# A bidirectional scan block on one core: the main loop written as a table of 24 pairs, with matmuls of like tile shape put together

## The chip, the core and the metric

The kernel runs on one core of a Trainium2 chip. A core has TensorE (matmuls, PE in the profile, with PEld for its weight loads), VectorE (DVE), ScalarE (ACT), GpSimd (POOL) and SyncE (SP, which here issues nearly all DMAs). The metric is device microseconds from start to end of one execution. The median of 3 runs before the change is 1835.07 us (1831.49 to 1840.69).

## What is computed

The input x is (4, 128, 96, 96): batch, channels, image. A group norm over 32 groups comes first. Each image is then read as a sequence of 9216 positions in four directions (rows forward and back, columns forward and back), and each sequence goes through the same block:

```python
t = grouped1x1(x, in_proj_w, in_proj_b, 4)        # 128 -> 512 channels
u, gate = t[:, :256], t[:, 256:]
u = silu(u)
u = depthwise_conv(u, dw_w)                       # 5 taps along the sequence
s = conv1x1(u, ssm_in_w)                          # 256 -> 32
a = 0.999 + 0.0009 * sigmoid(conv1x1(u, ssm_delta_w, ssm_delta_b))
bb = tanh(conv1x1(u, ssm_b_w, ssm_b_b)); cc = tanh(conv1x1(u, ssm_c_w, ssm_c_b))
prefix = cumsum(log(a))
hst = exp(prefix) * cumsum(bb * s * exp(-prefix))
u = u + conv1x1(cc * hst + ssm_d * s, ssm_out_w)  # 32 -> 256
u = grouped1x1(u * sigmoid(gate), mix_w, mix_b, 4)
y = conv1x1(u, out_proj_w, out_proj_b)            # 256 -> 128
```

The four directions' outputs are put back in image order, joined (4 x 128 channels), multiplied by fuse_w (512 -> 128), and added to x.

## The kernel before

mix, out_proj and fuse are linear and follow each other, so at the start they are multiplied into one weight, w_fin, one for each direction. The decay and the cumulative sums are one recurrence, h = a*h + b*s, done by VectorE's scan.

**Work units.** There are 8 phases: for each of 4 images first the columns (V), then the rows (H). A phase runs two directions at once, the streams s = 0 and s = 1, one of which is read backwards. It has 6 steps (st) of 1536 positions, and a step is cut by position modulo R = 4 into four parts p of N = 384 columns. A *pair* is both streams of one part: 24 pairs to a phase, 192 in all. Channels are on the partitions; the 256 hidden channels are two halves j.

In the second half of a phase the two streams meet the stretches that the other one has already read. silu outputs and gates are then not computed again: they were written to DRAM (`kept_sil`, `kept`) and are loaded back. `fresh(step)` is true in the first half; `mirror(n)` is not None for pairs whose gates are loaded.

**A pair's way through the engines**, with its lines:

- in_proj (`in_proj`, matmuls by the helper `mm`, L134): 32x32 tiles of the array, 16 for each pair. `silu` L495 on ScalarE. Only in fresh steps, four pairs ahead.
- convolution of the first 128 channels on TensorE. Positions are interleaved by 4, so a five-tap window touches two columns of four-position blocks. `conv` multiplies the block that holds most taps (128x32 tiles, weights `band`); `conv_less` the block that holds the others (64x32 tiles, weights `less`). For p = 0 and p = 3 only one of the four positions of that second block has a tap, for p = 1 and 2 two have. ScalarE copies the result to `u` (L632, L634).
- convolution of the other 128 channels as five taps: the first on ScalarE (L649), four on VectorE (L651), in the PSUM banks TAPS = 0 and 1.
- `proj`: the four small projections (128x32 tiles), then tanh, copy, tanh on ScalarE (L683, L684, L689); `decay` L691 and a product L692 on GpSimd; `scale_s` L701 on ScalarE; `scan` L718 on VectorE.
- six pairs later (LAG): `outputs` L724, L725, L727 on GpSimd; `under` L528 copies u into the banks SSM = 0 to 3; `out_of` L520 adds ssm_out to it (32x128 tiles, four products); where gates are computed, `gate` L514 (32x128 tiles) and tanh L537; `gating` L600 on VectorE multiplies. Banks 0 and 1 serve both the taps and stream 0's ssm_out.
- one pair later still: `accumulate`, sixteen w_fin matmuls in two banks (128x32 tiles), ScalarE copies to `ys` (L751, L753), GpSimd adds it to the image accumulator `acc` (L770).

**What sets the order.** The order is written by hand (`manual_schedule`): every engine runs its instructions in the order in which the code issues them. `pair(t)` issues everything of one turn: convolution and projection of pair t, in_proj of pair t + 4, gates and ssm_out of pair t - 6, w_fin of pair t - 7. Its branches `with_front`, `old`, `ahead` choose between three arrangements, and `late` one at a change of batch, when `acc` has to be sent and loaded anew. `start()` computes the statistics and the first step; `tail()` finishes the last pairs. The statistics of the next batch are computed in small pieces in between (`stats_finish`, a generator that `stats_piece` advances).

At the start SP issues the loads of x (`load_x`), whose chunks VectorE takes statistics of (L282); ScalarE's queue issues the weights small, fuse and main. `stay_busy` are matmuls whose result is not used.

## Time and profile before

| | us |
|---|---|
| median of 3 runs | 1835.07 |
| profiled execution, run time | 1833.3 |
| its span | 1831.6 |
| TensorE busy | 1806.8 |
| ScalarE busy | 1566.0 |
| VectorE busy | 1448.8 |
| GpSimd busy | 1423.5 |

The span runs from the first to the last instruction; the run's time also holds what lies around it. Busy times of different engines lie beside each other. The granted TensorE clock was 0.996 over the span. A row of the page such as

```profile
L520 PE MATMUL psum<-t,main 32*128 32x384 f32 x1536 | 241.9, 513 | 3.3 <-ACT psum L528 2.6
```

reads: line, engine, operation, output and inputs, the tile of the array (rows * columns), shape, count; then busy time in us and the mean of one in ns; then idle time of the engine just before, and what ended most of it. A matmul of the program stands in this trace as two records (768 ssm_out products, 1536 records). The mean of one says little, since tiles of the array work at the same time: what counts is from the start of one group to the start of the next.

### The profile page before, as it was taken

The page shows a single profiled execution, that of the slowest core. Times are in us where ns is not written, and L with a number is a line of the kernel's source. Part 1 is how long each engine was busy: PE and PEld are TensorE (multiplying, and loading weights), DVE is VectorE, ACT ScalarE, POOL GpSimd, SP SyncE. Part 2 cuts the span into 40 slices and gives each one's busy share as a digit, 9 for nine tenths or more (in the row PEclk, how much of TensorE's full clock was granted, in tenths as well). Part 3 has the DMA queues.
Part 4 walks back from the last instruction along what each step waited for, and adds up shares of the span by engine and source line. Part 5 has one row for each costly group of instructions (what it writes and reads, how often), then busy time and mean ns, then how long its engine had stood idle before and what let it go on. Part 6 is the DMA issues. An engine that isn't in the chain of part 4 may idle for free.

```text
span 1831.6 us, 57282 instructions
## 1 busy us (share of the span) xinstructions
PE 1806.8 (99%) x24068; PEld 653.9 (36%) x24068; DVE 1448.8 (79%) x1451; ACT 1566.0 (86%) x2762; POOL 1423.5 (78%) x1469
## 2 busy tenths in 40 slices
PE   7999999999999999999999999999999999999998
PEld 4333333333333333333333333333333333333333
DVE  5888878877878888877778888877877778777886
ACT  4888888988888888888898888888888888888975
POOL 2487887778777888787877888787877788887785
PEclk8999999999999999999999999999999999999999
DMA  6755563444965566244696546443476634535434
GB/s 196 200 191 179 164 192 108 161 144 147 307 227 181 167 188 190 102 142 140 214 296 207 165 162 211 136 152 110 162 236 223 234 123 152 192 109 179 148 122 156
DMA packets 147825, 321.18 MB, mean 175 GB/s; under 512 B 14192, under 2 KB 115696, under 8 KB 147568
## 3 DMA queue, kind: packets, MB, share of 16 engines
q1 hardware_dynamic: 147136, 316.56, 53.1%
q8 instruction: 190, 3.11, 0.7%
q10 hardware_dynamic: 432, 0.96, 0.1%
q14 instruction: 67, 0.55, 0.1%
HBM read 185.21 MB, written 132.25 MB: 173 GB/s over the span
## 4 chain that ended last, share of the span: by engine, by line
PE 96%; ACT 2%; DMA 1%; DVE 1%; issue 0%; SPq 0%; POOL 0%; ACTq 0%; DVEq 0%; POOLq 0%
PE psum L134 82%; PE psum L520 8%; PE psum L514 5%; ACT sil L495 0%; DMA x_in<-in_xs 0%; DMA fuse<-in_fuse 0%; PE psum L286 0%; DVE u L600 0%; ACT t L701 0%; ACT t L689 0%; PE psum L364 0%; ACT psum L649 0%; DMA out<-acc 0%; ACT u L632 0%; DVE psum L651 0%
## 5 line engine op out<-in xcount | busy, mean ns | idle before, releaser
L651 DVE SCALAR_TENSOR_TENSOR psum<-sil,small,psum 128x768 f32<-128x768 f32 x576 | 588.9, 1022 | 33.2 <-ACT psum L649 7.4
L600 DVE SCALAR_TENSOR_TENSOR u<-gate,psum 128x768 f32<-128x768 f32 x376 | 349.6, 952 | 256.6 <-ACT gate L537 118.6
L134 PE MATMUL psum<-u,w_fin 128*32 128x384 f32 x6176 | 551.7, 487 | 0.2 <-ACT t L689 0.2
L134 PE MATMUL psum<-u,main 128*32 128x384 f32 x6144 | 536.4, 490 | 0.1
L770 POOL TENSOR_TENSOR acc<-ys,acc 128x384 f32<-128x384 f32 x374 | 412.2, 1122 | 33.3 <-ACT ys L751 9.1
L724 POOL TENSOR_TENSOR t<-t,t 64x384 f32<-64x384 f32 x191 | 234.9, 1230 | 158.4 <-PE psum L514 78.8
L134 PEld LDWEIGHTS psum<-u,w_fin 128*32 128x32 f32 x6176 | 189.1, 110 | 320.8 <-issue 218.7
L134 PEld LDWEIGHTS psum<-u,main 128*32 128x32 f32 x6144 | 181.6, 110 | 327.6 <-issue 199.1
L528 ACT COPY psum<-u 128x768 f32<-128x768 f32 x352 | 276.9, 800 | 20.7 <-DVE u L651 10.2
L691 POOL TENSOR_SCALAR t<-tm 64x384 f32<-64x384 f32 x191 | 177.0, 927 | 151.0 <-ACT tm L683 100.8
L134 PE MATMUL psum<-sil,band 128*32 128x384 f32 x3072 | 286.8, 489 | 3.1 <-ACT ys L753 3.1
L725 POOL TENSOR_TENSOR t<-t,t 64x384 f32<-64x384 f32 x191 | 246.4, 1290 | 15.0
L520 PE MATMUL psum<-t,main 32*128 32x384 f32 x1536 | 241.9, 513 | 3.3 <-ACT psum L528 2.6
L649 ACT ACTIVATE psum<-sil,small 128x768 f32<-128x768 f32 x192 | 174.1, 907 | 63.2 <-DVE u L600 53.7
L537 ACT ACTIVATE gate<-psum,bnorm 128x384 f32<-128x384 f32 x384 | 192.6, 582 | 28.9 <-PE psum L514 26.9
L692 POOL TENSOR_TENSOR t<-t,tm 64x384 f32<-64x384 f32 x192 | 195.0, 1016 | 15.4 <-ACT t L684 0.2
L651 DVE SCALAR_TENSOR_TENSOR u<-sil,small,psum 128x768 f32<-128x768 f32 x192 | 194.9, 1015 | 7.8
L495 ACT ACTIVATE sil<-psum,bnorm 128x385 f32<-128x385 f32 x384 | 191.7, 584 | 3.6 <-PE psum L134 1.4
L134 PE MATMUL psum<-sil,less 64*32 64x384 f32 x3072 | 168.2, 495 | 0.0
L514 PE MATMUL psum<-x_in,wn 32*128 32x384 f32 x768 | 162.0, 528 | 2.3 <-ACT u L632 1.2
L753 ACT COPY ys<-psum 128x384 f32<-128x384 f32 x281 | 129.9, 476 | 30.2 <-PE psum L134 29.2
L134 PEld LDWEIGHTS psum<-sil,band 128*32 128x32 f32 x3072 | 90.2, 109 | 175.6 <-issue 94.1
(92 smaller groups left out, 1500.3 us busy)
## 6 DMA issues: line engine op xcount, KB each, us to landing
sil<-sil SPq DMA_DIRECT2D x128, 770.0 KB, 6.7
kept<-gate SPq DMA_DIRECT2D x80, 768.0 KB, 3.7
gate<-kept SPq DMA_DIRECT2D x76, 768.0 KB, 5.2
x_in<-in_xs SPq DMA_DIRECT2D x192, 96.2 KB, 2.4
out<-acc SPq DMA_DIRECT2D x48, 384.0 KB, 8.0
acc<-in_xr SPq DMA_DIRECT2D x38, 384.0 KB, 6.9
xs<-in_xr SPq DMA_DIRECT2D x72, 192.0 KB, 4.7
x_in<-in_xs SPq DMA_DIRECT2D x184, 48.1 KB, 3.7
```

Source lines behind the costliest of these rows:

```text
L134: nc.tensor.matmul(o[r, : rhs.shape[-1]], lhsT, rhs, start=start, stop=stop, skip_group_check=True)
L495: nc.scalar.activation(sils[step][:, s, j, g, :], bank(bk)[:, : N + 1], AF.Silu, bias=bn[:, 1:2] if j else bn[:, 4 + g : 5 + g],)
L514: nc.tensor.matmul(bank(to)[:, :N], stats[un["b"]][0][r, s, :], x_in[s][r, q, off : off + N], start=True, stop=True)
L520: nc.tensor.matmul(bank(SSM + 2 * s + j)[:, :N], w_so[r, bass.ts(j, P)], z[r, :], start=bi not in seeded, stop=True, skip_group_check=True)
L528: nc.scalar.copy(psum[:, SSM + 2 * s : SSM + 2 * s + 2, :N], us[bi][:, s])
L537: nc.scalar.activation(gv[:, s, j, :], bank(to[2 * s + j])[:, :N], AF.Tanh, bias=bn[:, 2 + j : 3 + j], scale=0.5,)
L600: nc.vector.scalar_tensor_tensor(v, g, 1.0, pz, ALU.add, ALU.mult)
L651: nc.vector.scalar_tensor_tensor(us[i][:, :, 1, :] if k == K - 1 else part, src, w_tap[:, k : k + 1], part, ALU.mult, ALU.add,)
L692: nc.gpsimd.tensor_mul(ta[0:64, p, :], tb[0:64, :], tm[0:64, :])
L724: engine.tensor_mul(ta[0:64, p, :], tb[64:P, :], ta[64:P, p, :])
L725: engine.tensor_add(tb[0:64, :], ta[0:64, p, :], tb[0:64, :])
L770: adder.tensor_add(part, y, part)
```

## The change

The turns t = 6 to 187 are no longer issued by `pair(t)` but read from a table. `ORDER` has 24 rows, one for each pair of a phase; each token is an operation and the pair it belongs to, relative to the row: B0, B1 (conv of a stream), L (conv_less of both), CU (copy to u), FT, T1 to T4 (taps), P (a product of proj), TA, CS, TC (its evictions), DE, BS, SC, SN (decay, product, scale_s, scan), CH, AD, CZ (outputs), X and Z (in_proj and silu), G and H (gate and its tanh), U, S, V (under, ssm_out, gating), A (an add in place of under), W, Y, Q (w_fin, its eviction, its add to acc), BN (statistics). `BANKS` gives each row's PSUM banks and two flags, whether ssm_out and gates are issued as four pieces of 32 columns or as one of 128. `middle()` walks the table, `work()` issues one token. Turns 0 to 5 and 188 to 191, `start()` and `tail()` stay as they were, apart from what is shown.

The order of p within a step becomes (0, 3, 1, 2) in the first half of a phase and (1, 2, 0, 3) in the second. The rows of the array that p = 0 and p = 3 use in `conv_less` are laid out (`ROWS`) so that the two streams of both lie on four different groups of 32 rows; these products are now 32x32 tiles (`lone`), and those of p = 1 and 2 stay 64x32. The weights of the convolution, 22 blocks, are laid out by the host (`band_of`) accordingly.

w_fin's adds (Q) go through a list `held`, which is emptied at once except near a change of batch, where up to three wait. acc is sent and loaded in one piece a turn. `ys` gets 6 buffers in place of 2, `u` one more. At the start the loads of fuse and main move to SP's queue, main behind all of x; the next step's first rows are loaded before the second burst of in_proj; the four `stay_busy(512)` go; the bias product sums w_of and w_fuse over the directions on GpSimd first, so that it has 3 matmuls in place of 12.

```diff
+YS = 6
+FIRST, LAST = 6, 188
+LAGS = {**dict.fromkeys("XZ", -R), **dict.fromkeys("SGHUVA", LAG), **dict.fromkeys("WYQ", LAG + 1)}
+TURNS = ((1, 2, 0, 3), (0, 3, 1, 2))
+ROWS = (((1, 0, 3, 2), (3, 2, 1, 0)), ((0, 1, 2, 3), (2, 3, 0, 1)))
...
+ORDER = (
+    (
+        "B0+1 B1+1 LO+1 DE-1 U1-6 T1 T2 T3 CU+1 LO SC-1 B1 B0 W0-7 T4 CU Q1-8 SN X11+4 X00+4 "
+        "U0-6 X10+4 S10-6 S00-6 S01-6 S11-6 V0-6 Y0-7 Z00+4 CH-5 X01+4 V1-6 P10 P11 Z10+4 "
+        "FT+1 T1+1 T2+1 T3+1 Q0-7 TC Z11+4 AD-5 P00 P01 CS Z01+4 W1-7 TA W0-6 CZ-5 DE Y1-7 "
+    ),
+    (
+        "T4 Q1-8 W1-7 U1-6 Y0-7 SN X00+4 U0-6 Y1-7 S10-6 Z00+4 S11-6 X10+4 X01+4 S00-6 S01-6 "
...
+BANKS = (
+    ((4, 7), (4, 7), (5, 2), (7, 5, 4, 6), (), 1, 1),
...
-            for p in range(R):
+            for turn, p in enumerate(TURNS[st < NS // 2]):
...
-    w_out_fuse = load(fuse, "fuse", pp)
-    load_x([(10, 4)])
-    w_main = load(main, "main")
-    load_x([(14, 4), (18, 4), (22, 2)])
+    w_out_fuse = load(fuse, "fuse", pp, nc.sync)
+    load_x([(10, 4), (14, 4), (18, 4), (22, 2)])
+    w_main = load(main, "main", wp, nc.sync)
...
-        low = 64 * ((less_of(p) + s + 1) % 2)
-        return slice(low, low + 64)
-
-    band = wp.tile([P, 2, R, 4, 32], F32, name="band")
-    less = wp.tile([P, R, 4, 32], F32, name="less")
+        return half(s if p == 1 else 1 - s)
+
+    bands = wp.tile([P, 22, 4, 32], F32, name="band")
+    band = bands[:, 0:16].rearrange("p (f s e) g m -> p f s e g m", f=2, s=2)
+    less = bands[:, 16:20].rearrange("p (f s) g m -> p f s g m", f=2)
+    lone = bands[:, 20:22]
...
+    shape = [P, 4, 32]
+    for e in (8, 12, 21, 11, 15, 9, 13, 18, 19, 10, 14, *range(8), 16, 17, 20):
+        nc.gpsimd.tensor_mul(
+            bands[:, e],
+            id32.unsqueeze(1).broadcast_to(shape),
+            w_dw[:, e, :].unsqueeze(2).broadcast_to(shape),
+        )
...
-    terms = [(w_of[:, d, j, :], b_mix[:, j : j + 1]) for d in range(4) for j in range(2)]
-    terms += [(w_fuse[:, d, :], b_out) for d in range(4)]
+    for w in (w_of, w_fuse):
+        for e in (2, 1):
+            nc.gpsimd.tensor_add(w[:, 0:e], w[:, 0:e], w[:, e : 2 * e])
+    terms = [(w_of[:, 0, j, :], b_mix[:, j : j + 1]) for j in range(2)]
+    terms += [(w_fuse[:, 0, :], b_out)]
...
-    for _ in range(4):
-        stay_busy(512)
...
+        if step > 1 and step % NS != 1:
...
+    def conv_less(i, banks, first=(False, False)):
         step, p = units[i]["step"], units[i]["p"]
-        sil, k, b0 = blocks(step), less_of(p), min(banks)
+        sil, k, f = blocks(step), less_of(p), fresh(step)
         for g in range(4):
             for s in range(2):
-                r = less_rows(s, p)
-                mm(bank(b0 + s), g, less[r, p, g, :], columns(step, sil[s][r, g, :], k),
-                   False, True)
-        if banks == PROJ:
+                if p in (0, R - 1):
+                    row = ROWS[f][s][p]
+                    r = slice(32 * row, 32 * row + 32)
+                    w = lone[r, f, g, :]
+                else:
+                    r = less_rows(s, p)
+                    w = less[r, f, s, g, :]
+                mm(bank(banks[s]), g, w, columns(step, sil[s][r, g, :], k), first[s],
+                   not first[s])
...
+        us[i] = wk.tile([P, 2, 2, N], F32, tag="u", bufs=LAG + 3, name=f"u_{units[i]['id']}")
...
+            ys = wk.tile([P, N], F32, tag="ys", bufs=YS, name=f"ys_{bu['id']}")
...
+    def piece(o, cols, lhsT, rhs, start):
+        nc.tensor.matmul(o[cols, : rhs.shape[-1]], lhsT[:, cols], rhs, start=start, stop=True,
+                         skip_group_check=True)
+
+    def split(small):
+        return [slice(32 * c, 32 * c + 32) for c in range(4)] if small else [slice(0, P)]
...
+        elif kind == "L":
+            conv_less(i, conv_b, [first_of("conv", n, q) for q in range(2)])
+        elif op == "CU":
+            copy_u(i, conv_b)
...
+        elif kind == "S":
+            r = slice(64 * j + 32 * s, 64 * j + 32 * s + 32)
+            for cols in split(s_small):
+                piece(bank(SSM + 2 * s + j), cols, w_so[r, bass.ts(j, P)], tbs[i][r, :], i not in seeded)
...
+        elif kind == "G":
+            q, off = gate_at(units[i])
+            r = slice(64 * (1 - s) + 32 * j, 64 * (1 - s) + 32 * j + 32)
+            for cols in split(g_small):
+                piece(bank(g_b[2 * s + j]), cols, stats[units[i]["b"]][0][r, s, :],
+                      x_in[s][r, q, off : off + N], True)
...
+        elif kind == "W":
+            final_mm(units[i + e], w_b[e])
+        elif kind == "Y":
+            while held and len(adds) >= YS:
+                add_held()
+            adds[n, e] = summand(units[i + e], w_b[e])
...
+        elif kind == "Q":
+            held.append((n, e))
+            turn = 2 * (n % (NU // 2 // B)) + e
+            while len(held) > (max(0, min(turn + 1, 3, 6 - turn)) if n >= NU // 2 // B else 0):
+                add_held()
+        elif kind == "X":
+            step, g = divmod(n, R)
+            in_proj(step, g, s, j, x_b[2 * s + j])
...
+    def slot_begins(t):
+        m = t + R
+        step, g = divmod(m, R)
+        if step * UB < NU and not fresh(step):
+            front(m, None)
+        for n in soon:
+            load_kept(n)
+        soon.clear()
+        if t % (NU // 2 // B) == 0:
+            load_chunks(t + 2)
+        reload_acc(1)
+        send(1)
...
+    def middle():
+        for t in range(FIRST - 2, LAST + 2):
+            if FIRST <= t < LAST:
+                plan_of.append(("", 0, t))
+            for token in ORDER[t % NP].split():
+                op, sign, n = token.partition("+") if "+" in token else token.partition("-")
+                n = t + int((sign + n) or 0)
+                if belongs(op, n):
+                    plan_of.append((op, n, t_of(op, n)))
+        while plan_of:
+            op, n, t = plan_of.popleft()
+            if op:
+                if next_kind[0] is False and free[0] in banks_of(op, t):
+                    stats_piece(False, True)
+                work(op, n, t)
+            else:
+                slot_begins(t)
...
+        for s in range(2):
+            load_front(1, s, slice(64 * s, 64 * s + 32), slice(0, R))
...
-        for t in range(NU // 2):
+        for t in range(FIRST):
+            pair(t)
+        middle()
+        waiting[:] = units[2 * (LAST - LAG - 1) : 2 * (LAST - LAG)]
+        for t in range(LAST, NU // 2):
```

## The prediction

> **What bounds the kernel now.** I read the page's busy shares first, then the chain that ended last, then TensorE's timeline over one pair of each kind.
>
> ```profile
> PE 1806.8 (99%) x24068; PEld 653.9 (36%) x24068; DVE 1448.8 (79%) x1451; ACT 1566.0 (86%) x2762; POOL 1423.5 (78%) x1469
> PE 96%; ACT 2%; DMA 1%; DVE 1%; issue 0%; SPq 0%; POOL 0%; ACTq 0%; DVEq 0%; POOLq 0%
> ```
>
> The first line is busy time by engine, the second the chain by engine: TensorE is the chain nearly throughout, so a microsecond taken from it counts until another engine is late. A busy TensorE need not be a full one; the timeline (start, length, engine, line, instructions) shows what it is busy with. A pair with an in_proj and kept gates:
>
> ```profile
> 244.75 2.79 PE L134 MATMUL psum<-u,main 128*32 128x384 f32 x32
> 247.47 0.95 PE L134 MATMUL psum<-x_in,wn 32*32 32x385 f32 x32
> 248.35 1.50 PE L134 MATMUL psum<-sil,band 128*32 128x384 f32 x16
> 249.66 2.76 PE L134 MATMUL psum<-u,w_fin 128*32 128x384 f32 x32
> 252.36 0.88 PE L134 MATMUL psum<-sil,less 64*32 64x384 f32 x16
> 253.16 0.93 PE L520 MATMUL psum<-t,main 32*128 32x384 f32 x8
> 254.02 2.79 PE L134 MATMUL psum<-u,main 128*32 128x384 f32 x32
> ```
>
> A pair that computes gates:
>
> ```profile
> 330.82 2.79 PE L134 MATMUL psum<-u,main 128*32 128x384 f32 x32
> 333.43 1.47 PE L134 MATMUL psum<-sil,band 128*32 128x384 f32 x16
> 334.72 1.47 PE L134 MATMUL psum<-u,w_fin 128*32 128x384 f32 x16
> 336.12 0.88 PE L134 MATMUL psum<-sil,less 64*32 64x384 f32 x16
> 336.93 1.50 PE L134 MATMUL psum<-u,w_fin 128*32 128x384 f32 x16
> 338.36 0.59 PE L514 MATMUL psum<-x_in,wn 32*128 32x384 f32 x2
> ...
> 339.94 0.53 PE L134 MATMUL psum<-u,main 128*32 128x384 f32 x4
> ```
>
> I count in passes: one pass is the whole array filled once with 384 columns, so four 128x32 tiles, eight 64x32, four 32x128 or sixteen 32x32. The program's 12034 matmuls stand in the trace as two records each, so eight records of 128*32 are a pass. Band to w_fin, 333.43 to 334.72, is two passes of one shape: 1.29 us, 0.645 each. The first pair takes 254.02 - 244.75 = 9.27 us for 13 passes (8.385), so 0.885 us goes to its five changes of tile shape, 0.177 each. The second takes 9.12 for 13 passes with four changes, 0.184 each. So a change of shape costs 0.18 us, and a small product alone in its shape about 0.81 to 0.88 us for 0.645 of work.
>
> **What the Trainium skill says.** "TensorEngine Tiling (Array Packing)", Tiling Modes, says that a change of tiling mode drains the engine while tiles of one mode run independently; the 0.18 us per change agrees. Its Restrictions and Gotchas add that different row tiles must not write one PSUM bank at once; the new table's bank lists keep them apart. "ScalarE: Activation LUTs", What ACT_TABLE_LOAD costs, says that back-to-back ACTIVATEs overlap by about 93 ns. The trace agrees: four silus in a row take 2.00 us, one alone 0.58, so 0.11 is lost per silu that is set apart.
>
> **The change part by part.** Counting tile shapes in the order of both programs gives 2509.0 passes and 867 visits (runs of one shape) before, 2455.7 and 640 after.
>
> *Small conv products.* Pairs with p = 0 and p = 3 now read only the 32 rows in which they have a tap. Both pairs' sixteen 32x32 tiles cover the array once: one pass instead of two, 48 passes over 192 pairs, 48 x 0.645 = 31.0 us. Pairs with p = 1 and 2 keep a full pass each but share a visit.
>
> *in_proj with ssm_out.* Both are now 32x32 in most slots (an ssm_out product as four pieces), so their two passes form one visit; gates with ssm_out stay two passes. Over four pairs 20 changes become about 12 where in_proj runs and 16 become about 12 where gates do. All visits together: 867 - 640 = 227 changes x 0.18 = 40.9 us. No visit of two 32x32 passes is in the trace. The nearest is the gate and ssm_out visit in 32x128: 339.94 - 338.36 = 1.58 us, 0.29 above its two passes instead of 0.18. There are 96 such two-pass visits now and 166 afterwards (126 of them 32x32), so I add 70 x 0.11 = 7.7 us. The bounds: 0 if 32x32 packs better than that; and if each of the 126 costs 0.24 more (what an in_proj visit of one pass, 0.88, holds above 0.645), 30 us.
>
> *The ordering table.* No arithmetic is added on ACT, DVE or POOL: taps, under-copies, silus, gates, scans, the three POOL steps and the adds keep their number. So their load per pair must now fit in a shorter pair. Four pairs cost TensorE 51 passes and 12 changes, 32.9 + 2.2 = 35.1, or 8.8 us a pair. The windows view over eight to ten pairs of each kind:
>
> ```profile
> 102.30:175.20 72.90, 72.90 (x904) 27.09 (x900) 60.55 (x61) 65.28 (x113) 60.88 (x57) 1.00 0.56 188
> 421.50:514.40 92.90, 83.13 (x152) 1.00 0.79 252
> ```
>
> Columns are PE, PEld, DVE, ACT, POOL in the first; the second is ACT alone. ACT is busy 83.13 / 10 = 8.31 us per in_proj pair and 65.28 / 8 = 8.16 per gate pair: 95% and 93% of 8.8. DVE needs 7.6 and POOL up to 8. One ring is as tight: taps and ssm_out share banks 0 and 1, so one pair's four taps (4.15 us of DVE), the under-copy (0.8), ssm_out, gating (0.95) and the next first tap (0.91) follow each other. In the trace it closes in 9.27 with about 1.2 us of queueing, so 8.1 bare, and up to 0.6 more when ssm_out sits inside a two-pass visit. The cover is there, but thin. Engines at 93 to 100% that wait for each other in a fixed order lose something: at least nothing, at most the whole gain of the in_proj pairs (a rival below). I take 1% of a pair, 0.088 x 182 table pairs = 16 us.
>
> *Held adds, 6 ys buffers, one more u buffer, SP.* One row shows what a batch change costs TensorE today:
>
> ```profile
> L134 PE MATMUL psum<-sil,band 128*32 128x384 f32 x3072 | 286.8, 489 | 3.1 <-ACT ys L753 3.1
> ```
>
> The last two columns are busy time with mean, and idle time before with its releaser: 3.1 us, three waits of 1.05, one per change of batch, where a pair's products were queued behind a ys copy. With six ys buffers they go, 3.1 us back. The held adds (1.12 us each) shift on POOL, which has a fifth to spare. SP's DMAs move as well (acc reloads one per pair instead of four together, silu stores skipped in some steps and done later); the queues are busy 53%, so I cost this 0, upper end 4 us should a gate or silu load be late behind a waiting store.
>
> *The start.*
>
> ```profile
> 15.86 5.38 PE L286 MATMUL psum<-w_fin 128*128 128x512 f32 x8
> 21.07 0.28 PE L187 MATMUL psum<-mv,gmean 128*128 128x1 f32 x2
> 37.28 2.16 PE L134 MATMUL psum<-x_in,wn 32*32 32x385 f32 x32 [2.81 <-DMA x_in<-in_xs]
> ```
>
> The four filler matmuls go. The statistics were aggregated by 20.22 (19.42 + 0.80) yet their matmul began at 21.07 behind the fillers: 0.85 back. VectorE waited 3.4 us for x chunks that shared the DMA engines with fuse and main; with main last, perhaps 1.5 returns. Loading the next step's rows before the second burst removes most of the 2.81, but the product behind needs VectorE's last tap (ends 37.0), so 2. Against it: fuse comes later and POOL's 22 band products (0.40 each) now precede four added sums of w_of and w_fuse before the bias product. Together 0.85 + 1.5 + 2 = 4.4 us gain, 0 to 7. The last four pairs and the tail keep their old code.
>
> Sum against the profiled span: 1831.6 - 31.0 - 40.9 + 7.7 + 16 - 3.1 - 4.4 = 1775.9. The profiled run took 1833.3, 1.7 more than its span, and the median of the runs is 1.8 above that: 1779.
>
> **Rivals.**
> *Full gain:* the order fits, no added waits, two-pass visits cost one change: 1779 - 16 - 7.7 = 1755. For it: ACT and DVE have slack in gate pairs. Against: 95% on ACT.
> *ScalarE sets the in_proj pairs:* silus set apart cost 4 x 0.11 more, 8.31 + 0.44 = 8.75, plus its waits of 0.5 us for gating (the first tap is held by it now), 9.2 a pair against 9.27 before; the 80 or so pairs with in_proj and old gates keep their time and only gate pairs gain: 1779 + 80 x (9.2 - 8.8) = 1811.
> *Slower, the bank 0 and 1 ring:* ssm_out waits inside the merged visit for in_proj tiles whose banks ScalarE has not freed, the gating, first tap and taps come late, and TensorE, in order, stands. The ring decides once ssm_out stands 1.2 us longer than the bare 8.1, that is above 9.3; at 9.6 a pair in all 182, 0.4 over the former mean of 9.2, it gives 1835 + 73 - 4 = 1904, and in in_proj pairs alone about 1865. For it: ring, ACT and TensorE are within 8% of each other. Against: the table pulls the first taps ahead of the products in several slots.
> *It doesn't do what it says:* the small products of two pairs run one after the other; 31 us stay, 1810.
>
> **How the numbers follow.** Forecast (1763 to 1797 by itself) 0.63; full gain 0.13; ScalarE 0.11; ring 0.08; no overlap 0.05. The 8-in-10 range goes from 1755 to 1812, from the full gain to just past the ScalarE case. No change is within 0.5% of 1835, 1826 to 1844: only stragglers of the ScalarE and ring cases, 0.04. Slower 0.07, faster 0.89.
>
> **What would show it.** In the changed profile: products of two pairs' small rows in 32*32 within about 0.85 us; in_proj with ssm_out in about 1.6 us; TensorE's matmul records rise (pieces), yet its span falls; four pairs in about 35 to 35.8 us; ACT above 87%. Wrong if TensorE's idle time exceeds some 40 us, with waits on ACT (under-copy, silu) ending most of it, or if 32*32 visits of two passes take 1.9 us or more.

## The result, and the profile after

The changed kernel is slower, by 1.35%. Its median is 1860.7 us (1856.5 to 1863.9) against 1834.4 for the kernel before on the same chip: ratio 1.0135, 95% interval 1.0111 to 1.0159. The profiled execution spans 1859.8 us, 28.2 more than before. The forecast was 1779.

First the page of the kernel after: busy time by engine, then the chain that ended last by engine.

```profile
PE 1803.4 (97%) x28410; PEld 670.4 (36%) x28410; DVE 1458.8 (78%) x1451; ACT 1546.0 (83%) x2765; POOL 1476.0 (79%) x1479
PE 69%; DVE 13%; ACT 8%; POOL 7%; issue 2%; DMA 1%; SPq 0%; DVEq 0%; POOLq 0%; ACTq 0%
```

TensorE's busy time is nearly that of before (1806.8 us), yet the chain is TensorE for only 69% of the span where it was 96%. The rest runs through VectorE, ScalarE and GpSimd: TensorE now waits for them in many places. Part of this shows as idle time, 56.4 us (1859.8 - 1803.4) against 24.8 before, 10.6 of it the wait for the load of fuse at the start. The rest the busy share hides, because a wait that falls inside a visit (a run of one tile shape) is covered by the records of the matmuls that are still under way.

TensorE's timeline (start, length, engine, line, names, instructions) over a pair with an in_proj shows the new visit:

```profile
214.23 1.47 PE L290 MATMUL psum<-u,w_fin 128*32 128x384 f32 x16
215.63 0.53 PE L290 MATMUL psum<-x_in,wn 32*32 32x385 f32 x4
215.65 0.60 PE L1100 MATMUL psum<-t,main 32*32 32x384 f32 x12
...
216.94 0.70 PE L290 MATMUL psum<-x_in,wn 32*32 32x385 f32 x12
217.57 2.79 PE L290 MATMUL psum<-u,main 128*32 128x384 f32 x32
220.17 4.05 PE L290 MATMUL psum<-u,w_fin 128*32 128x384 f32 x48
224.16 0.53 PE L1100 MATMUL psum<-t,main 32*32 32x384 f32 x4
...
226.06 2.79 PE L290 MATMUL psum<-u,main 128*32 128x384 f32 x32
```

The long products run at their old rate: 217.57 to 220.17 is four passes in 2.60 us. The two passes of in_proj with ssm_out, however, take 217.57 - 215.63 = 1.94 and 226.06 - 224.16 = 1.90 us. Before, the two stood apart at 0.88 and 0.86, 1.74 together. So the change of shape that was saved brought nothing here; the merged visit is longer than the two were.

To count this over the program I matched every TensorE record (two a matmul) with its tile shape, and took a visit from its first record to the next visit's. The 126 two-pass visits in 32x32 have a median of 1.93 us (tenth to ninetieth percentile 1.90 to 2.07). The small conv products of two pairs in one 32x32 pass take 0.88 (median), where the forecast had about 0.85.

The waits view of the kernel after (engine, its instruction, what it waited for; us in total, times, longest) names what the other engines wait for:

```profile
DVE u L766 <- PE psum L1100: 134.1, 63, 5.6
POOL t L1145 <- ACT t L1137: 80.0, 47, 5.5
ACT psum L824 <- DVE u L766: 63.9, 104, 1.2
ACT t L876 <- POOL t L1145: 50.2, 70, 2.5
PEld psum L1100 <- ACT psum L689: 19.4, 50, 1.7
```

Gating (L766) waits for ssm_out, ScalarE's first tap (L824) for gating, GpSimd's product (L1145) for ScalarE, and ScalarE's scale_s (L876) for GpSimd; where ssm_out (L1100) waits for ScalarE's under-copy (L689), the circle of engines closes, each engine in a fixed order. Such waits alone do not show what sets the pace, for the kernel before has them too. The same view of it:

```profile
DVE u L600 <- ACT gate L537: 118.6, 80, 3.2
ACT psum L649 <- DVE u L600: 53.7, 90, 1.8
DVE u L600 <- PE psum L520: 36.6, 22, 3.4
```

What is new is that gating waits for ssm_out (134.1 against 36.6 us) more than for the gate's tanh, and that scale_s waits at all: the kernel before has no wait put down to it.

Where the 28.2 us lie: from the first w_fin product of one phase (a batch in one direction, 24 pairs) to that of the next, the kernel before takes 222.0, 225.2, 221.4, 225.2, 221.5, 225.2, 220.4 us, the kernel after 230.7, 222.9, 228.9, 222.8, 229.0, 223.8, 222.8. The first, third and fifth phases lose 7.5 to 8.7. They also gather the next batch's statistics. The others lose little or gain. The last phase adds 5.2 and the start 3.0. Inside the second phase eight pairs that compute gates take 76.2 against 74.0 us, eight of those with an in_proj 73.2 against 74.2. It is so in all phases: eight gate pairs take 76.2 to 78.4 us against 72.9 to 74.0, so it is mainly the gate pairs that lose.

### The profile page after: what moved, and what is told of

Read it like the earlier page. It is cut to its first block, busy times and chain, and to the rows that moved or that the text cites. A ratio compares the mean times of both kernels' runs of the same rounds, so it can differ in the third digit from the quotient of the medians.

```text
span 1859.8 us, 65548 instructions
## 1 busy us (share of the span) xinstructions
PE 1803.4 (97%) x28410; PEld 670.4 (36%) x28410; DVE 1458.8 (78%) x1451; ACT 1546.0 (83%) x2765; POOL 1476.0 (79%) x1479
## 4 chain that ended last, share of the span: by engine, by line
PE 69%; DVE 13%; ACT 8%; POOL 7%; issue 2%; DMA 1%; SPq 0%; DVEq 0%; POOLq 0%; ACTq 0%
PE psum L290 58%; PE psum L1100 10%; DVE psum L826 6%; DVE t L893 3%; DVE u L766 2%; POOL acc L950 2%; ACT psum L824 2%; ACT psum L689 2%; DVE u L826 2%; POOL t L1145 1%; POOL t L1143 1%; POOL t L1167 1%; ACT sil L656 1%; ACT t L1139 1%; PE psum L681 1%
## 5 line engine op out<-in xcount | busy, mean ns | idle before, releaser
L766 DVE SCALAR_TENSOR_TENSOR u<-gate,psum 128x768 f32<-128x768 f32 x376 | 346.0, 951 | 230.6 <-PE psum L1100 134.1
L950 POOL TENSOR_TENSOR acc<-ys,acc 128x384 f32<-128x384 f32 x374 | 427.8, 1148 | 72.0 <-ACT ys L933 34.2
L290 PE MATMUL psum<-sil,band 128*32 128x384 f32 (+2 forms) x6144 | 404.8, 492 | 2.9 <-ACT t L864 1.3
L1100 PE MATMUL psum<-t,main 32*32 32x384 f32 (+1 forms) x4480 | 311.1, 494 | 15.0 <-ACT psum L689 7.0
L1145 POOL TENSOR_TENSOR t<-t,tm 64x384 f32<-64x384 f32 x182 | 205.0, 1126 | 148.1 <-ACT t L1137 80.0
L689 ACT COPY psum<-u 128x768 f32<-128x768 f32 x352 | 282.4, 805 | 38.3 <-DVE u L826 26.1
L1163 POOL TENSOR_TENSOR t<-t,t 64x384 f32<-64x384 f32 x182 | 240.2, 1320 | 32.8 <-DVE t L893 19.7
L1165 POOL TENSOR_TENSOR t<-t,t 64x384 f32<-64x384 f32 x182 | 251.7, 1383 | 7.9
L824 ACT ACTIVATE psum<-sil,small 128x768 f32<-128x768 f32 x192 | 174.2, 907 | 71.2 <-DVE u L766 63.9
L656 ACT ACTIVATE sil<-psum,bnorm 128x385 f32<-128x385 f32 x384 | 205.2, 578 | 22.7 <-PE psum L290 15.6
L290 PEld LDWEIGHTS psum<-sil,band 128*32 128x32 f32 (+2 forms) x6144 | 123.4, 107 | 263.7 <-issue 217.2
L1143 POOL TENSOR_SCALAR t<-tm 64x384 f32<-64x384 f32 x182 | 190.9, 1049 | 27.7 <-ACT tm L1135 13.4
L290 PE MATMUL psum<-x_in,wn 32*32 32x385 f32 x3072 | 165.6, 505 | 5.5 <-DVE mean L347 1.8
L1100 PE MATMUL psum<-x_in,wn 32*32 32x384 f32 (+1 forms) x2112 | 169.2, 499 | 1.6 <-ACT u L809 1.2
L876 ACT ACTIVATE t<-t,small 64x384 f32<-64x384 f32 x192 | 117.5, 612 | 50.6 <-POOL t L1145 50.2
```

Of the source, the lines that this page charges most:

```text
L290: nc.tensor.matmul(o[r, : rhs.shape[-1]], lhsT, rhs, start=start, stop=stop, skip_group_check=True)
L656: nc.scalar.activation(sils[step][:, s, j, g, :], bank(bk)[:, : N + 1], AF.Silu, bias=bn[:, 1:2] if j else bn[:, 4 + g : 5 + g],)
L689: nc.scalar.copy(psum[:, SSM + 2 * s : SSM + 2 * s + 2, :N], us[bi][:, s])
L766: nc.vector.scalar_tensor_tensor(v, g, 1.0, pz, ALU.add, ALU.mult)
L824: nc.scalar.activation(part, src, AF.Copy, scale=w_tap[:, 0:1])
L950: adder.tensor_add(part, y, part)
```

## The experiments

All ratios are to the kernel before on the same chip, with 95% intervals; "visits" was run once and has no ratio.

| run | median us | ratio | interval |
|---|---|---|---|
| after | 1860.7 | 1.0135 | 1.0111 to 1.0159 |
| before_pieces | 1862.5 | 1.0150 | 1.0124 to 1.0175 |
| after_whole_gates | 1860.9 | 1.0138 | 1.0118 to 1.0158 |
| after_apart | 1911.4 | 1.0411 | 1.0388 to 1.0433 |
| before_half_fin | 1741.3 | 0.9483 | 0.9431 to 0.9535 |
| after_half_fin | 1842.9 | 1.0038 | 1.0026 to 1.0051 |
| after_two_taps | 1843.8 | 1.0043 | 1.0027 to 1.0059 |
| whole_two_taps | 1843.9 | 1.0036 | 1.0023 to 1.0049 |
| half_two_taps | 1807.0 | 0.9846 | 0.9817 to 0.9876 |
| after_sc_later | 1867.2 | 1.0172 | 1.0144 to 1.0199 |
| half_sc_later | 1849.7 | 1.0072 | 1.0044 to 1.0101 |
| after_cz_first | 1863.2 | 1.0140 | 1.0119 to 1.0160 |
| after_no_stats | 1844.9 | 1.0041 | 1.0026 to 1.0055 |
| whole_s_last | 1900.0 | 1.0343 | 1.0325 to 1.0360 |
| whole_taps_no_scale | 1831.2 | 0.9968 | 0.9956 to 0.9980 |
| sc_whole_filler | 1862.5 | 1.0141 | 1.0115 to 1.0167 |
| cz_whole_filler | 1856.5 | 1.0112 | 1.0087 to 1.0137 |
| s_last_cz_filler | 1902.2 | 1.0346 | 1.0324 to 1.0368 |

### Are the merged visits slow by themselves?

**visits** measures TensorE alone: four passes in 128x32, then one visit of a kind, repeated with no other engine taking part (the block itself is left out). This is the visit of two 32x32 passes:

```diff
+    def two():
+        for e in range(2):
+            for r, c in order:
+                nc.tensor.matmul(bank(4 * e + r)[rc(c, 32), :384], wt[rc(r, 32), rc(c, 32)], data[r][rc(r, 32)], **flags)
```

> Leaves out the whole block: after the weights it only issues visits of small tiles, each between four passes in 128x32, and writes x back. From the start of a visit to the start of the 128x32 group behind it: if a 32x32 visit of two passes is slow by itself (about 30 ns for each of its 64 records, since 16 records at a time seem to be under way), one pass 0.88 us, two 1.9, three 2.9 to 3.0, two with the tiles issued across the row groups 1.9 as well, two in 64x32 1.45, two in 32x128 1.5 to 1.6, one in 32x32 and one in 32x128 behind it 1.7 to 1.75. If the order of row groups makes it slow: two across the row groups 1.6 or less. If it is slow in the changed kernel only because operands come late: two 1.5 to 1.6 and three 2.2 here.

TensorE's timeline in this run; L399 is the filling product, L408 two passes in 32x32, L424 two in 64x32, L429 two in 32x128, L433 with L435 one pass each in 32x32 and 32x128:

```profile
65.18 1.92 PE L408 MATMUL psum<-acc,w_fin 32*32 32x384 f32 x64
67.04 2.79 PE L399 MATMUL psum<-acc,w_fin 128*32 128x384 f32 x32
...
206.58 1.52 PE L424 MATMUL psum<-acc,w_fin 64*32 64x384 f32 x32
208.03 2.79 PE L399 MATMUL psum<-acc,w_fin 128*32 128x384 f32 x32
...
214.92 1.57 PE L429 MATMUL psum<-acc,w_fin 32*128 32x384 f32 x16
216.42 2.79 PE L399 MATMUL psum<-acc,w_fin 128*32 128x384 f32 x32
...
248.68 0.94 PE L433 MATMUL psum<-acc,w_fin 32*32 32x384 f32 x32
249.55 0.93 PE L435 MATMUL psum<-acc,w_fin 32*128 32x384 f32 x8
250.41 2.79 PE L399 MATMUL psum<-acc,w_fin 128*32 128x384 f32 x32
```

Start to start, two passes take 1.86 us in 32x32, 1.45 in 64x32 and 1.50 in 32x128. One and three passes in 32x32 take 0.87 and 2.69, and another order of the row groups leaves two passes at 1.85. One 32x32 and one 32x128 visit apart take 0.87 + 0.86 = 1.73: *less* than the two merged in 32x32. So beyond the first pass a 32x32 pass costs 0.84 to 0.98 us where other shapes take about 0.645, with no other engine involved. The Trainium skill, "TensorEngine Tiling (Array Packing)", Overview, gives sixteen independent 32x32 tiles and up to 16 times as the theoretical maximum of such tiling; here, with 384 columns of f32, they keep up two thirds to three quarters of the rate of four 128x32 tiles (0.645 over 0.98 and over 0.84). A 32x32 pass has sixteen matmuls where the others have four or eight; whether their number or the shape itself costs the time, no run separates.

**before_pieces** puts only this into the kernel before: gates and ssm_out of the 96 gate pairs as 32x32 pieces.

```diff
-        nc.tensor.matmul(bank(to)[:, :N], stats[un["b"]][0][r, s, :], x_in[s][r, q, off : off + N],
-                         start=True, stop=True)
+        for c in range(4):
+            mm(bank(to), c, stats[un["b"]][0][r, s, 32 * c : 32 * c + 32],
+               x_in[s][r, q, off : off + N], True, True)
```

> The kernel before, with gates and ssm_out of the 96 gate pairs issued as four pieces of 32x32 each, nothing else moved. If two passes of 32x32 take 1.93 by themselves: 96 x (1.93 - 1.58) = 34 us slower, ratio 1.018. If the long visits come from waits of the table: 0 to 10 us, ratio up to 1.005.

It costs 1.5%, 28 us, 0.29 for each of the 96 pairs. That this equals the loss of the whole change is chance: the new table has other visits in pieces. Its two-pass visits take 1.90 instead of 1.58, so in the old order the pieces are paid almost in full.

**after_whole_gates** takes the pieces out of the new table's gate rows (the two flags in BANKS; one of seven rows is shown), **after_apart** makes all gate and ssm_out products whole and groups in_proj and ssm_out apart in the order of ten rows. In three of these it also puts ScalarE's eviction of w_fin (Y) ahead of an under-copy.

```diff
-    ((4, 5), (4, 5), (7, 6), (), (4, 5, 6, 7), 1, 1),
+    ((4, 5), (4, 5), (7, 6), (), (4, 5, 6, 7), 0, 0),
```

> The changed kernel, with gates and ssm_out issued whole (32x128) in all rows that compute gates; same order. If two passes of 32x32 are slow by themselves: 53 visits x (1.93 - 1.58) = 18 us faster than the changed kernel, 1842. If waits fill the visits: no more than 5 us, 1855 to 1861.

> As after_whole_gates, and in the rows with in_proj the four ssm_out products are whole and stand together before or behind the four in_proj products, so that each has a visit of its own again. If two passes of 32x32 are slow by themselves: a further 73 x (1.93 - 0.88 - 0.86) = 14 us, about 1828. If a shared visit is worth a change of shape, as forecast: 73 x 0.18 = 13 us slower than after_whole_gates.

Neither wins the loss back. With whole products the gate visits still take 1.90 us (median of 97), because an ssm_out product inside them waits for ScalarE's under-copy. The trace shows it: of the 95 such visits behind 100 us, 81 have the end of an under-copy inside them, and they end 1.30 to 1.42 us after it (tenth to ninetieth percentile) however late it is; the 14 others take 1.58 to 1.64, as before the change. In the kernel after, that wait was in the shade of the slow pieces. Priced with the times that "visits" gives, TensorE's work between 100 us and the tail falls by some 20 us, and its waits rise by about as much. after_apart is worse by 50 us. Its in_proj visits, now alone, take 1.45 us (median) against 0.88 before the change, so waits fill them too, and its order on ScalarE differs: the run shows that this order does not work, not what a visit apart is worth.

### What sets the pace?

These runs leave work out to see whose time counts. **before_half_fin** and **after_half_fin** leave out the second half (j = 1) of the w_fin product in the main loop, two passes a pair, 248 us of TensorE at 0.645. **after_two_taps** and **whole_two_taps** leave out two of VectorE's four taps (2.04 us a pair; whole_two_taps has the gate rows of after_whole_gates). **half_two_taps** leaves out both in the kernel after.

```diff
-        for j in range(2):
+        for j in range(1):
...
+            if k in (2, 3):
+                continue
```

> The kernel before without the second half (j = 1) of every w_fin product in its 192 pairs' main loop: two passes of TensorE less a pair, 248 us of its own work in all; nothing else moves. TensorE was the only bound, so the time falls until ScalarE (8.2 to 8.3 us a pair) is the next: 1620 to 1680.

> The changed kernel, with the same half of every w_fin product left out. If TensorE's slow 32x32 visits set the pace of the table: it falls with TensorE like the kernel before, to 1620 to 1690. If the fixed order of the other engines (taps, under-copies and gating round banks 0 and 1, or ScalarE's queue) sets it: it keeps most of its time, 1780 to 1850.

> The changed kernel without taps 2 and 3 on VectorE (2.05 us of a pair's four taps); TensorE and ScalarE keep all their work. If the ring through banks 0 and 1 (taps, under-copy, ssm_out, gating, first tap) holds the table up: it falls to what TensorE's visits need, 1795 to 1820. If ScalarE's or GpSimd's order or the slow visits do: less than 15 us, 1845 to 1860.

> The changed kernel with whole gates and ssm_out in the gate rows, and without taps 2 and 3. If the ring hid the gain of the whole products: their 18 us show now, 1777 to 1802, some 18 us under after_two_taps. If not the ring: equal to after_two_taps within 5 us.

> Leaves out the second half of the output product (two passes a pair) and two of the four taps of VectorE together. Each alone brought some 17 us. If TensorE and VectorE each cover for the other (the ring needs both shorter, whichever is longer shows), both together give far more than the sum of 35: 1700 to 1790 us. If a third thing sets the pace, the order of ScalarE's and GpSimd's queues, they give no more than their sum: 1815 to 1835 us, and the chain of waits then runs through ScalarE and GpSimd for more than half of the span.

The chain that ended last, first of before_half_fin:

```profile
PE 69%; ACT 14%; DVE 9%; DMA 4%; issue 2%; POOL 1%; SPq 0%; ACTq 0%; DVEq 0%; POOLq 0%
```

of after_half_fin:

```profile
PE 39%; ACT 24%; DVE 22%; POOL 9%; issue 4%; DMA 1%; SPq 0%; DVEq 0%; POOLq 0%; ACTq 0%
```

and of half_two_taps:

```profile
PE 40%; ACT 25%; POOL 18%; DVE 9%; issue 5%; DMA 2%; SPq 0%; POOLq 0%; DVEq 0%; ACTq 0%
```

The same 248 us of TensorE are worth 95 us in the old order and 18 in the new one (1842.9 against 1860.7). Even the old order gives back less than forecast: 1741 where 1620 to 1680 was expected. Two taps are worth 17 us, between the two bands, and 17 to 19 with whole gates: by the test set down for whole_two_taps the ring is not what hid the gain of the whole products. Both together are worth 54, more than the sum of 35, and 1807 lies between the two bands of half_two_taps; ScalarE and GpSimd have 43% of its chain, not more than half.

The reading that fits these runs is that the new table has several circles of nearly one length: TensorE's own work, the ring of taps, under-copy, ssm_out and gating, and something through ScalarE and GpSimd. Shortening one shows the next within 1%. That these are the circles, and all of them, is not shown. TensorE's side is seen in after_half_fin: the two-pass 32x32 visits grow from 1.93 to 2.40 us (median), and the named wait of ssm_out for the under-copy, 7.0 us in the kernel after, grows to 49.1:

```profile
PE psum L1100 <- ACT psum L689: 49.1, 50, 2.3
```

### Which waits?

**after_sc_later** issues scale_s one pair later, so that its 50.2 us of waiting hold nothing behind them; **half_sc_later** does it with half the w_fin product.

```diff
-        "CU+1 L B0 B1 T1 T2 T3 W0-7 U1-6 T4 SC-1 U0-6 SN X00+4 CU Y0-7 S01-6 S11-6 S10-6 "
-        "S00-6 X10+4 V0-6 X11+4 Z00+4 Z10+4 FT+1 CH-5 X01+4 P00 V1-6 P01 P11 P10 AD-5 Q0-7 "
+        "CU+1 L B0 B1 T1 T2 T3 W0-7 U1-6 T4 U0-6 SN X00+4 CU Y0-7 S01-6 S11-6 S10-6 "
+        "S00-6 X10+4 V0-6 X11+4 Z00+4 Z10+4 FT+1 CH-5 X01+4 SC-1 P00 V1-6 P01 P11 P10 AD-5 Q0-7 "
```

> Only one ScalarE instruction a pair is moved: scale_s (0.5 us, in the kernel after it waits 50.2 us in 70 places for GpSimd's product L1145) is issued one pair later, just before the next pair's projection, instead of right behind that product. Theory 'order of ScalarE's queue': these waits stand at the head of ScalarE's queue and hold the u copies and under-copies behind them, and with them the ring of under-copy, ssm_out and gating: 1820 to 1840 us, ratio to the kernel before 0.992 to 1.003, the 50 us row gone and the 134 us row of gating waiting for ssm_out smaller by more than 20. Rival 'slow pieces': TensorE's slow 32x32 visits set the pace and ScalarE's wait is in their shade: 1855 to 1862 us.

> Leaves out the second half of the output product (two passes a pair, as in after_half_fin) and also issues scale_s one pair later. With TensorE's work out of the way the run shows what the order of the other engines costs. Theory 'order of ScalarE's queue': clearly below after_half_fin's 1843, at 1790 to 1825 us. Rival 'ring of banks 0 and 1' (taps, under-copy, ssm_out, gating whatever ScalarE waits for elsewhere): within 8 us of 1843.

Nothing is gained; both medians are some 6 us above their base, with intervals that overlap. ScalarE's wait for GpSimd was in the shade of others.

**after_cz_first** puts GpSimd's copy CZ, which ssm_out reads, ahead of held adds in twelve rows. This place of the kernel after suggested it (the last column is idle time and its releaser):

```profile
342.96 0.19 PEld L1100 LDWEIGHTS psum<-t,main 32*128 32x128 f32 x3 [1.91 <-POOL t L1167]
```

```diff
-        "AD-6 Q1-8 Q0-8 P01-1 P00-1 TA-1 BS-1 CZ-6 W0-7 W1-7 G01-6 U1-6 T1 T2 T3 T4 SN Y0-7 "
+        "AD-6 CZ-6 Q1-8 Q0-8 P01-1 P00-1 TA-1 BS-1 W0-7 W1-7 G01-6 U1-6 T1 T2 T3 T4 SN Y0-7 "
```

> Only GpSimd's order is changed: the copy CZ (L1167, 0.53 us), whose result four ssm_out products read, comes directly behind the add AD that feeds it, ahead of the held adds (1.15 us each) and of the product BS, in eight rows of the table with CZ-6 and in rows 9, 11, 12, 15, 16, 18, 20 and 21 with CZ-5. In the kernel after, comparing every TensorE visit with the tenth percentile of its kind, row 9 loses 1.5 to 3.5 us a phase (the wait for L1167 at 342.96 us is 1.91) and rows 13 and 17 some 0.6 and 0.5 to 1.1, so about 8 x 2.3 = 18 us stand behind late GpSimd copies. Theory 'a few places where an instruction was put too late in a queue, each costing what TensorE waits there': 18 us less than after, 1840 to 1848. Rival 'the whole order is a ring, and a wait that is removed comes back elsewhere' (as with whole gates and with scale_s later): 1855 to 1862.

TensorE's visits show why nothing is gained. In the phases of the second direction the loss in row 9 falls from 1.5 to 0.5 us, but 0.6 us appears thirteen pairs later that was not there, and in the later phases of the first direction row 9 loses 2.4 to 3.6 us instead of 1.7 to 2.0. The expected 18 us did not come.

**after_no_stats** leaves out the statistics of the second to fourth batch and uses the first batch's for all.

```diff
-        if un["order"] == "V" and b < B and k > 1:
+        if False:
...
-        wn = stats[units[step * UB]["b"]][0]
+        wn = stats[b0][0]
```

> Leaves out the statistics of the second to fourth batch (their chunk loads, 72 statistics instructions of VectorE at 0.55 us, and the pieces of the group norm); all batches use those of the first. Phases with statistics last 229 to 231 us in the kernel after and the one V phase without 222.8; in the kernel before 221.5 and 220.4. Theory 'the statistics have no room in the new order, whose visits wait for VectorE's pieces': 18 to 24 us less than after, 1837 to 1843. Rival 'VectorE has slack enough (78% busy), the V phases lose by their memory layout or accumulations': within 6 us of after.

The ratio falls by 0.0094, 17 us, and all seven phases take 222.7 to 224.2 us, just short of the 18 to 24 us expected. In the kernel before, phases with statistics take some 1.2 us more than the one without, in the kernel after 6.7: over three phases 16 to 17 us of the loss. The pieces of the group norm stand in VectorE's and TensorE's queues, and TensorE waits for them. Two lines of TensorE's weight loads in the kernel after, at in_proj products whose bank a statistics product used:

```profile
714.51 0.13 PEld L290 LDWEIGHTS psum<-x_in,wn 32*32 32x32 f32 x5 [1.27 <-DVE mean L347]
754.96 0.13 PEld L290 LDWEIGHTS psum<-x_in,wn 32*32 32x32 f32 x5 [1.28 <-DVE bnorm L400]
```

**whole_s_last** changes only TensorE's order inside the gate visits of after_whole_gates: the gate products first, ssm_out last. One of ten rows, in part and wrapped anew:

```diff
-        "U0-6 Y0-7 H01-6 H00-6 G10-6 S10-6 G11-6 S00-6 S11-6 S01-6 H10-6 H11-6 V0-6 P01 P00 "
+        "U0-6 Y0-7 H01-6 H00-6 G10-6 G11-6 S10-6 S00-6 S11-6 S01-6 H10-6 H11-6 V0-6 P01 P00 "
```

> after_whole_gates with TensorE's order changed inside one visit: in the ten rows 8 to 17 the four gate products go first and the four ssm_out products behind them (in the table they alternate, and an ssm_out product that waits for ScalarE's under-copy L689 holds the gate products queued behind it). With whole products such visits took 1.89 to 2.05 us in the table against 1.58 in the kernel before. Theory 'the wait sits inside the visit, in front of ssm_out': visits back to about 1.6, some 80 x 0.35 = 28 us less than after_whole_gates' 1861: 1828 to 1840. Rival 'the ring through banks 0 and 1 sets the pair's time, the wait only moves': 1853 to 1862.

The opposite of the expectation: 39 us slower. One such visit, with what stands in it (ACT is ScalarE):

```profile
367.16 0.46 ACT L836 COPY ys<-psum 128x384 f32<-128x384 f32 x1
367.51 0.80 ACT L592 COPY psum<-u 128x768 f32<-128x768 f32 x1
367.67 0.92 PE L1003 MATMUL psum<-x_in,wn 32*128 32x384 f32 x6
368.25 0.58 ACT L834 ACTIVATE ys<-psum,b_fin 128x384 f32<-128x384 f32 x1
368.87 0.18 PEld L1003 LDWEIGHTS psum<-x_in,wn 32*128 32x128 f32 x1 [0.90 <-ACT ys L834]
370.36 0.16 PEld L193 LDWEIGHTS psum<-u,main 128*32 128x32 f32 x8 [0.55 <-ACT gate L596]
370.59 0.95 DVE L669 SCALAR_TENSOR_TENSOR u<-gate,psum 128x768 f32<-128x768 f32 x1 [3.30 <-PE psum L1003]
```

The last gate product waits for ScalarE's ys copy (L834), whose bank it needs, so now ssm_out behind it waits for that copy too; the visit takes 370.36 - 367.67 = 2.69 us against 2.05 in after_whole_gates, and gating stands 3.30 us. Over the program 75 of 95 such visits are longer, most by 0.64 us, 46 us in all, and 39 of them reach the end: there is little slack around ssm_out.

**whole_taps_no_scale** leaves scale_s out of whole_two_taps.

```diff
         elif op == "SC":
-            scale_s(i)
+            pass
```

> whole_two_taps (gates and ssm_out whole, two of the taps left out) with scale_s of the table's pairs left out as well: 0.61 us of ScalarE a pair, and its wait for GpSimd's product. In whole_two_taps the under-copy that ssm_out waits for starts 1.35 us (median) after the last tap, and ScalarE has no gap before it in 23 of 23 pairs: its own queue holds it. Theory 'ScalarE's queue is the next bound, of nearly the same length as the ring and as TensorE's work': the under-copy comes earlier, 20 to 40 us less than 1844: 1804 to 1824. Rival 'it is GpSimd or the fixed order of something else': 1836 to 1846.

It gains 12.7 us, between the two bands. In the second phase the under-copy still starts 1.37 us (median) after the last tap, so scale_s is not what holds it back, and the reason given is not shown. The run shows only that scale_s on ScalarE, with its wait for GpSimd, costs time once taps and pieces are relieved.

### Versions meant to beat both

**sc_whole_filler** joins scale_s later, whole gates and the four filler products back at the start, **cz_whole_filler** CZ first instead of scale_s later, and **s_last_cz_filler** the order of whole_s_last to that.

```diff
+    for _ in range(4):
+        stay_busy(512)
```

> A version meant to beat both: scale_s one pair later, gates and ssm_out as whole 32x128 products in the ten rows that compute gates, and the four filler products of the kernel before put back at the start. Theory 'order of ScalarE's queue': after_sc_later less some 20 us that whole gate products free (they freed 21 us of TensorE in after_whole_gates, all lost to waits) and less 3 to 4 us at the start: 1800 to 1820 us. Rival 'something else holds the order': 1850 to 1860 us, with only the start's 3 to 4 us gained.

> The copy CZ first as in after_cz_first, gates and ssm_out as whole 32x128 products in the ten rows with gates, and the four filler products of the kernel before at the start: meant to beat both. If the waits are single places: after's 1861 less 18, less some 20 for whole products, less 4 at the start: 1815 to 1828, ratio to before 0.988 to 0.996. If waits come back elsewhere: 1845 to 1857.

> The same order in cz_whole_filler (copy CZ first, whole products, fillers at the start), the version meant to beat both. Theory 'the wait sits inside the visit': 1856 less 28, 1824 to 1834, ratio to before 0.993 to 0.999. Rival 'ring': 1848 to 1857.

None does. The fillers themselves do answer, at the start. Two lines of the windows view over 21.5 to 35.2 us: after the length of the window stand the busy times of PE, PEld, DVE, ACT and POOL with their counts, then the granted TensorE clock (0.50 and 1.00 here), the DMA share and GB/s. The kernel after:

```profile
21.50:35.20 13.70, 13.70 (x183) 5.34 (x183) 2.85 (x18) 8.73 (x16) 0.00 (x0) 0.50 0.34 82
```

cz_whole_filler:

```profile
21.50:35.20 13.70, 12.89 (x222) 6.01 (x220) 4.13 (x23) 10.70 (x21) 0.00 (x0) 1.00 0.40 97
```

Without the fillers TensorE runs the first products at half clock; with them at full clock, and more gets done. The first w_fin product comes at 83.7 us in cz_whole_filler against 91.4 in after_cz_first, but at 92.0 in s_last_cz_filler against 93.1 in whole_s_last, so the gain is not steady, and in the medians it is at most 7 us.

## Why the prediction was wrong

Both kernels' TensorE, from its first visit to the start of its last, can be summed in three ways: at the prices of the forecast (0.645 a pass, 0.18 a visit), at those that "visits" and the profile of before give for each shape, and as the time that it took (us).

| | before | after | difference |
|---|---|---|---|
| at the forecast's prices | 1768.8 | 1693.6 | -75.2 |
| at the measured prices | 1763.1 | 1735.8 | -27.3 |
| taken | 1814.5 | 1838.6 | +24.1 |

With a first product that comes 3.8 us later and 0.3 at the end these are the 28.2. So, at these prices, 47.9 us went to slow shapes and 51.4 to new waits, some 47 of them behind 100 us.

- *Small conv products, -31.0:* right. Two pairs' products in one 32x32 pass take 0.88 us where two visits took 0.81 each. All of this gain lies in the first row of the table.
- *227 changes of shape, -40.9:* the count was right, the traces have 867 and 640 visits. It was not a saving where the merged visit is slower than the two apart: 1.86 us against 0.87 + 0.86 in "visits".
- *Two-pass visits, +7.7 with an upper end of 30:* the step that failed first. The 32x128 visit was taken as nearest (0.29 over two passes), and the upper end gave one more price of entry. Measured: 1.93 - 1.29 = 0.64 over, of which 0.57 (1.86 - 1.29) without any other engine. Against the 0.18 of any visit that is 0.39 each, 49 us over 126 visits, where this term of the sum had 7.7. The slow part is the second pass, 0.98 us, and the one-pass visits of the trace could not show it. The sign set down, "32*32 visits of two passes take 1.9 us or more", is there; the other, idle time above some 40 us mostly for ScalarE, is there in its size (56.4), but only some 22 of it end on ScalarE.
- *The ordering table, +16 for waits:* the second failure; 51.4 were measured. Engine loads per pair did fit (ScalarE 83% busy, though above 87% was set down as the sign), but fit is a mean. Some 17 us come from statistics that the load table, taken as means over pairs, did not place. What the other waits hang on is seen in part: an under-copy that comes late in the gate visits (after_whole_gates).
- *Batch changes, -3.1:* the row of w_fin and conv products no longer shows the 1.05 us waits; right.
- *Start, -4.4:* wrong sign, the first w_fin product comes 3.0 us later. The statistics' matmul did come 0.95 us earlier (20.12 against 21.07) and the 2.81 us stall is gone, but fuse ended its wait 3.8 us later (10.6 against 6.8) and the clock was half for 13.7 us; the fillers were costed as pure delay.
- *Rivals:* the slower one, the ring through banks 0 and 1, had 0.08 and 1865 in one form. Its links are in the waits view, but relieving the ring alone gave 17 us, so it is one of several and not the cause by itself. That its number is close is luck: the form that gave 1865 let the in_proj pairs lose, and it was mainly the gate pairs that lost. The ScalarE rival had it the other way round too, with a gain in gate pairs alone.

Shown: slow 32x32 passes (visits, before_pieces), the cost of statistics in the new order (after_no_stats), that ssm_out waits for a late under-copy (after_whole_gates), and that the table's pace hardly depends on TensorE's work alone (after_half_fin). Not shown: that the kernel would be faster without the slow passes, as taking them out of the gate rows changed nothing. Open: what makes the under-copy late, and which circle binds after each relief. Moving single instructions (scale_s, CZ) did not find it, and a version of the new table that beats the kernel before was not found.

## What to carry to other kernels

Price a merged visit by measuring that very shape and number of passes alone before building an order on it: here it would have shown that joining in_proj with ssm_out saves nothing. In a schedule in which four engines run at 78 to 97% in fixed orders, a saving on one engine can be worth little until the others have room; leaving out half of a product in both orders (95 against 18 us) tells how far TensorE sets the pace in each. Look for waits inside visits, which the busy share counts as work.

## What the runs showed of the hardware

- With f32 operands of 384 columns, a second pass of sixteen 32x32 tiles costs 0.98 us (1.85 - 0.87) and a third 0.84 (2.69 - 1.85), where a pass in 64x32 or 32x128 costs about 0.64 (1.45 - 0.81, 1.50 - 0.86).
- Without the fillers TensorE stayed at a granted clock of 0.50 for 13.7 us, although its records show it busy for all of them: the first in_proj burst of 96 records took 6.98 us instead of 3.85. It is no accident of one run. All thirteen traces of the new table without fillers have 13.7 or 17.1 us at half clock at this place and 6.98 or 6.99 for the burst; the six traces of whole kernels with fillers have 3.84 or 3.85 for it. The Trainium skill, "TensorE: Matmul & The Clock Gate", Part 1, lets the full clock come after about 3.4 us of sustained work; this start took at least four times as long. Why the clock stays down in this stretch, no run shows.
